# Filling the last stage's matrix products up to 128 rows and columns

## The chip, the cores and the metric

The kernel runs on one core of a Trainium2 chip. The metric is the device time of one execution in microseconds (us), as a median over runs. Beside it stands one profiled execution, from which every duration below comes. The engines are named as in the profile: PE is the matrix engine's multiplications, PEld its loads of the stationary operand, DVE the vector engine, ACT the scalar engine, POOL the GpSimd engine, SP the queue that issues the DMA transfers. In a matmul's shape, such as `64*128 64x96`, the first pair is the rows and columns of the array that the stationary operand fills, the second the moving operand.

## The reference

The input is `x` with 8 images of 64 by 64 pixels and 96 channels (C = 96), seen also as 8 sequences of 4096 tokens. Layer 0 is a state-space block with 192 inner channels (DI = 192); layer 1 is an attention without softmax and a small quantized network.

```
x = x + vss(group_norm(x))            # in_proj, 3x3 depthwise convolution, four selective scans,
                                      # y = layer_norm(y) * gamma + beta; y = y * silu(z)
                                      # out = y @ out_proj_w.T        (192 -> 96)
t = tokens(x)
t = t + attn(layer_norm(t))           # qkv = x @ Wqkv + bqkv; (q k^T) v for 6 heads; @ Wff + bff
t = t + ffn(layer_norm(t))            # q8(x) @ q8(W1) -> relu -> q8 -> @ q8(W2), 96 -> 384 -> 96
```

Without a softmax the attention is linear: q (k^T v) needs one product of the normalized tokens with themselves per sequence, the matrix `gram` of 97 by 97 with the constant 1 as a 97th channel, which carries the biases. It is multiplied with the weights into one matrix `weff` of 97 by 96, and each token's attention is one product with `weff`.

## The kernel before

Three stages follow each other: `pass1` (normalization, input projection, convolution), `pass2` (the scans, by far the longest) and `pass3`, which is what the change touches. `pass3` does everything from the layer norm after the scans to the output.

It works in units of 512 tokens (GRP), 8 units (UNITS) for each of 8 sequences, 64 in all. Inside a unit the tokens stand as 4 blocks (NU) of 128. A unit has a load and two parts:

- `load` (line 954) fetches the two scan directions `y` and `yo` with tokens on the partitions, the gate `zs` with channels on the partitions (128 channels in half 0, the remaining 64 in half 1), and the tokens `xr` for the residual.
- `first_part` (line 968) adds `y` and `yo` on POOL, standardizes on DVE, POOL and ACT (`standardize`, line 936), and transposes on PE: 4 transposes for channels 0 to 127 and 4 for channels 128 to 191 (64 columns of data). ACT copies each half out of PSUM with gamma and beta into `gt`, POOL multiplies it with `zs`. The product with `out_proj_w` runs, for each of the 4 blocks, over 128 rows with `w_out0` and then over 64 rows with `w_out1`, accumulating in the same PSUM tile. DVE adds the residual. The result is standardized into `ln` (96 channels, and POOL sets a 97th to 1), multiplied with itself into `pg`, and transposed into `lnT` (97 rows).
- `attention` (line 1021), once per sequence, makes `weff` from `pg`.
- `second_part` (line 1045), once the sequence's `weff` is there, multiplies `lnT` with `weff`, adds, standardizes into `lf`, transposes it into `xq` (96 rows, fp8), multiplies with `w1q` in three column blocks (`ph`), adds the bias and clips on DVE, quantizes on POOL (`hq`), multiplies with `w2q`, adds and stores.

A 32-bit product with `start`/`stop` as written appears in the trace as two matmul records with a stationary load each; a transpose is one record. So a unit has 16 records for `w_out`, 8 for `pg`, 8 for `weff`, 16 transposes (`tr`), 3 for `ph`, and 12 for `w2q`.

The order on each engine is fixed when the program is built. Each part is a generator that yields the engine and an assumed cost before each step; `weave` (line 142) plays all parts forward in assumed time and takes at each moment the step that could begin earliest. `InOrder` (line 83) chains the instructions of an engine in that order. At most five first and five second parts are open at a time (OPEN), and the second parts stand 12 units behind the first ones, so that the stage begins with first parts alone and ends with second parts alone. `Slots` and the tile pools count the buffers: 3 PSUM tiles for transposes, 2 for products, 2 for `ph`, 5 loads, 20 units held between the parts.

Of the kernel before, what the change touches and what calls it, by code (L numbers as in the profile page):

```python
# [33 lines left out]
F32 = mybir.dt.float32  # L34
F16 = mybir.dt.float16
BF16 = mybir.dt.bfloat16
F8 = mybir.dt.float8e5
AF = mybir.ActivationFunctionType
# [4 lines left out]
P = 128  # L43
NB, HH, WW, C = 8, 64, 64, 96
L = HH * WW
DI, N, R, K = 192, 16, 6, 4
# [12 lines left out]
GRP = 512  # L59
# [808 lines left out]
def pass3(ctx, tc, g, ident, mhalf, engines, y_d, z_d, out):  # L868
    nc = tc.nc
    pe, dve, act, pool = engines  # L870
    CA = C + 1
    sp = InOrder(tc, nc.sync)
    wp = ctx.enter_context(tc.tile_pool(name="p3w", bufs=1))
    one = ctx.enter_context(tc.tile_pool(name="p3one", bufs=1))
    two = ctx.enter_context(tc.tile_pool(name="p3two", bufs=2))

    OPEN = 5
    each = ctx.enter_context(tc.tile_pool(name="p3each", bufs=OPEN))

    LOADED, HELD = 5, 20  # L880
# [2 lines left out]
    held = ctx.enter_context(tc.tile_pool(name="p3held", bufs=HELD))  # L883
# [3 lines left out]
    ps_one = ctx.enter_context(tc.tile_pool(name="p3ps", bufs=1, space=PSUM))  # L887


    gb = wp.tile([P, 2, 2], F32, name="gb")  # L890
    for i, name in enumerate(("ln_gamma", "ln_beta")):
        nc.sync.dma_start(gb[:, 0, i : i + 1], g[name][0:P].unsqueeze(1))
        nc.sync.dma_start(gb[0 : DI - P, 1, i : i + 1], g[name][P:DI].unsqueeze(1))
    w_out0 = wp.tile([P, C], F32, name="w_out0")
    nc.sync.dma_start(w_out0, g["out_proj_wT"][0:P, :])
    w_out1 = wp.tile([DI - P, C], F32, name="w_out1")
    nc.sync.dma_start(w_out1, g["out_proj_wT"][P:DI, :])

    w_kv = wp.tile([CA, 2, C], F32, name="w_kv")
    nc.sync.dma_start(w_kv[0:C], g["Wqkv"][:, C:].rearrange("e (s c) -> e s c", s=2))  # L900
# [8 lines left out]
    nc.sync.dma_start(hmask, g["head_mask"])  # L909

    def load_quantized(shape, src, name):
        raw = one.tile(shape, F32, name=f"{name}_raw", tag="raw")
        nc.sync.dma_start(raw, src)
        q = wp.tile(shape, F8, name=name)
        nc.vector.tensor_copy(q, raw, saturate=False)
        return q

# [4 lines left out]
    nc.vector.tensor_copy(b1q, b1q8)  # L922
    b2q = load_quantized([P, C], g["b2"].unsqueeze(0).to_broadcast([P, C]), "b2q")

    NU = GRP // P
    UNITS = L // GRP
    done, counts = {}, {}
    loads, holds, grams, weffs = {}, {}, {}, {}

# [3 lines left out]
    def tokens(src, q):  # L933
        return src[q * GRP : (q + 1) * GRP].rearrange("(n p) c -> p n c", p=P)

    def standardize(src, dst, name, cost):

        yield "dve", 4 * cost
        st = each.tile([P, NU, 6], F32, name=f"st{name}")
        mv = each.tile([P, NU, 2], F32, name=f"mv{name}")  # L940
        for i in range(NU):
            dve.bn_stats(st[:, i, :], src[:, i, :])
        for i in range(NU):
            dve.bn_aggr(mv[:, i, :], st[:, i, :])
# [9 lines left out]
    def load(b, q):  # L954
        cols = slice(q * GRP, (q + 1) * GRP)
        end = yield "sp", 8.0, 5.0, slots["loaded"]
        y, yo = (loaded.tile([P, NU, DI], F32, name=name) for name in ("y", "yo"))
        for o, dst in enumerate((y, yo)):
            sp.dma_start(dst, tokens(y_d[b][o], q))
        zs = loaded.tile([P, 2, GRP], F32, name="zs")  # L960
        sp.dma_start(zs[:, 0, :], z_d[b][0:P, cols])
        sp.dma_start(zs[0 : DI - P, 1, :], z_d[b][P:DI, cols])
        xr = loaded.tile([P, NU, C], F32, name="xr")
        sp.dma_start(xr, tokens(g["x"][b], q))
        loads[b, q] = y, yo, zs, xr, slots["loaded"].taken
        done["load", b, q] = end

    def first_part(b, q):
        yield "load", b, q
        y, yo, zs, xr, of_loads = loads[b, q]  # L970
        yield "pool", 1.8, 0.3, slots["held"]
        t, lnT = held.tile([P, NU, C], F32, name="t"), held.tile([CA, GRP], F32, name="lnT")
        holds[b, q] = t, lnT, slots["held"].taken
        pool.tensor_add(y, y, yo)
        yield from standardize(y, y, "y", 0.45)
        for i, (ch, rows) in enumerate(((slice(0, P), P), (slice(P, DI), DI - P))):
            yield "pe", 0.6, 0.3, slots["tr"]
            pt, slot = take("tr", [P, GRP])
            for n in range(NU):
                pe.transpose(pt[0:rows, n * P : (n + 1) * P], y[:, n, ch], ident)  # L980
            end = yield ("act", 0.65) if i else ("act", 0.65, 0.3, slots["gates"])
            if i == 0:
                gt, of_gt = gates.tile([P, 2, GRP], F32, name="gt"), slots["gates"].taken
            act.activation(gt[0:rows, i, :], pt[0:rows, :], AF.Identity, bias=gb[0:rows, i, 1:2], scale=gb[0:rows, i, 0:1])
            slots["tr"].release(slot, end)
            yield "pool", 1.3
            pool.tensor_mul(gt[0:rows, i, :], gt[0:rows, i, :], zs[0:rows, i, :])
        end = yield "pe", 3.8, 0.3, slots["mm"]
        slots["gates"].release(of_gt, end)
        po, slot = take("mm", [P, NU, C])  # L990
        for i in range(NU):
            blk = slice(i * P, (i + 1) * P)
            pe.matmul(po[:, i, :], gt[:, 0, blk], w_out0, start=True, stop=False)
            pe.matmul(po[:, i, :], gt[0 : DI - P, 1, blk], w_out1, start=False, stop=True)
        end = yield "dve", 0.55, 0.0
        dve.tensor_add(t, po, xr)
        slots["mm"].release(slot, end)
        slots["loaded"].release(of_loads, end)
        ln = each.tile([P, NU, CA], F32, name="ln")
        yield from standardize(t, ln, "t", 0.35)  # L1000
        pool.memset(ln[:, :, C:CA], 1.0)
        if b > 0:
            yield "gram", b - 1
        end = yield "pe", 1.6
        if b not in grams:
            grams[b] = ps_one.tile([CA, CA], F32, name="pg")
        counts["gram", b] = counts.get(("gram", b), 0) + 1
        for i in range(NU):
            first, last = counts["gram", b] == 1 and i == 0, counts["gram", b] == UNITS and i == NU - 1
            pe.matmul(grams[b], ln[:, i, :], ln[:, i, :], start=first, stop=last)  # L1010
        if counts["gram", b] == UNITS:
            done["grams", b] = end
        yield "pe", 0.7, 0.3, slots["tr"]
        pl, slot = take("tr", [P, GRP])
        for i in range(NU):
            pe.transpose(pl[0:CA, i * P : (i + 1) * P], ln[:, i, :], ident)
        end = yield "act", 0.6
        act.copy(lnT, pl[0:CA, :])
        slots["tr"].release(slot, end)

    def attention(b):

        yield "grams", b
        end = yield "dve", 0.2
        gram = two.tile([CA, CA], F32, name="gram")
        dve.tensor_copy(gram, grams[b])
        done["gram", b] = end
        last = gram
        for rows, rhs, name in ((CA, w_kv[:, 1, :], "gv"), (C, w_kv[:, 0, :], "kvT"), (C, w_ff, "kvf"), (CA, None, "weff")):
            yield "pe", 0.7, 0.3, slots["mm"]  # L1030
            p, slot = take("mm", [P, NU, C])
            p = p[0:rows, 0, :]
            pe.matmul(p, last if rhs is not None else w_qT, rhs if rhs is not None else last, start=True, stop=True)
            end = yield "dve", 0.25
            last = two.tile([rows, C], F32, name=name)
            if name == "kvT":
                dve.tensor_mul(last, p, hmask)
            else:
                dve.tensor_copy(last, p)
            slots["mm"].release(slot, end)  # L1040
        dve.tensor_add(last[C:CA, :], last[C:CA, :], b_ff[C:CA, :])
        weffs[b] = last
        done["weff", b] = end

    def second_part(b, q):
        yield "weff", b
        t, lnT, of_hold = holds[b, q]
        end = yield "pe", 1.3, 0.3, slots["mm"]
        pa, slot = take("mm", [P, NU, C])
        for i in range(NU):  # L1050
            blk = slice(i * P, (i + 1) * P)
# [1 line left out]
        end = yield "dve", 0.55, 0.0  # L1053
        dve.tensor_add(t, t, pa)
        slots["mm"].release(slot, end)
        lf = each.tile([P, NU, C], F32, name="lf")
        yield from standardize(t, lf, "f", 0.35)

        yield "pe", 0.7, 0.3, slots["tr"]
        pf, slot = take("tr", [P, GRP])  # L1060
        for i in range(NU):
            pe.transpose(pf[0:C, i * P : (i + 1) * P], lf[:, i, :], ident)
        end = yield "dve", 0.7
        xq = each.tile([C, GRP], F8, name="xq")
        dve.tensor_copy(xq, pf[0:C, :], saturate=False)
        slots["tr"].release(slot, end)
        h1 = each.tile([P, NHC, GRP], F16, name="h1")
        for hc in range(NHC):
# [13 lines left out]
        po, slot = take("mm", [P, NU, C])  # L1082
# [17 lines left out]
    for b in range(NB):  # L1100
        units += [("first", b * UNITS + q - 12, first_part(b, q)) for q in range(UNITS)]
        units += [("load", b * UNITS + q, load(b, q)) for q in range(UNITS)]
        units.append(("attention", 0, attention(b)))
        units += [("second", b * UNITS + q, second_part(b, q)) for q in range(UNITS)]
    weave(units, {"load": 1, "first": OPEN, "attention": 1, "second": OPEN}, done)

# [44 lines left out]
```

## Time and profile before

| | |
|---|---|
| time, median of 3 runs | 10227.74 us (10223.3 to 10242.83) |
| time of the profiled execution | 10238.11 us |
| its span, first to last instruction | 10236.3 us |
| busy over the span: PE, PEld, DVE, ACT, POOL | 7669.6, 6320.8, 9578.9, 9152.3, 9194.7 us |
| mean clock granted to the matrix engine | 0.895 |
| last stage, from the last instruction of the scans | about 9331 to 10236 us of the span |

The page divides the span into 40 slices and gives for each the busy share of each engine in tenths and the clock that was granted to the matrix engine (1 is full). Times within the span are counted from the first instruction. All instructions that go through `InOrder` carry the line 91 of that helper, so groups are told apart by the names of their tiles: `mm<-w_out,gt` is the output projection, `tr<-ident,y` a transpose of `y`. Ends of matmuls are modelled; where the pace of a run of matmuls matters, it is read from the start of its first one to the start of the next group.

### The profile page before, as it was taken

How to read it: one execution, taken by the hardware profiler on the slowest of the kernel's cores; microseconds unless marked ns; L12 is line 12 of the kernel's file. 1: busy time of each engine (PE TensorE's matmuls, PEld its weight loads, DVE VectorE, ACT ScalarE, POOL GpSimd, SP SyncE). 2: the span in 40 equal slices, each digit the busy share in tenths (PEclk: the TensorE clock that was granted, in tenths of full speed). 3: DMA queues.
4: the chain of work that ended last, by engine and by line, in shares of the span. 5: the costliest groups of instructions: out<-in, count | busy, mean ns of one | idle time of the engine just before them, and what ended most of it. 6: DMA issues, size and time to landing. Idle time of an engine off the chain costs nothing.

```text
span 10236.3 us, 152471 instructions
## 1 busy us (share of the span) xinstructions
PE 7669.6 (75%) x52384; PEld 6320.8 (62%) x52384; DVE 9578.9 (94%) x6886; ACT 9152.3 (89%) x20499; POOL 9194.7 (90%) x3280
## 2 busy tenths in 40 slices
PE   7767777776777777777777777777777777776887
PEld 3336666665666666666666666666666666565775
DVE  7969999999999999999999999999999999996776
ACT  5669999999999999999999999999999999995665
POOL 1449999999999999999999999999999999997886
PEclk8889989989998989989989999999999899997776
DMA  5766776689976766799866666999667668996442
GB/s 165 236 209 217 229 228 221 228 209 206 211 221 212 224 218 216 223 205 205 221 210 223 219 214 225 209 204 213 216 213 230 210 226 210 206 208 169 125 126 60
DMA packets 928006, 2103.29 MB, mean 205 GB/s; under 512 B 274475, under 2 KB 422732, under 8 KB 925698
## 3 DMA queue, kind: packets, MB, share of 16 engines
q1 hardware_dynamic: 924426, 2092.18, 72.3%
q8 instruction: 420, 6.88, 0.3%
q14 instruction: 352, 2.88, 0.1%
q0 software_dynamic: 432, 0.94, 0.0%
q10 hardware_dynamic: 2376, 0.40, 0.0%
HBM read 1917.59 MB, written 175.66 MB: 204 GB/s over the span
## 4 chain that ended last, share of the span: by engine, by line
DVE 28%; ACT 26%; issue 15%; PE 15%; POOL 12%; DMA 3%; SPq 1%; DVEq 0%; ACTq 0%; POOLq 0%
DVE h L91 20%; ACT x L91 10%; ACT da L91 10%; POOL c L91 8%; PE acc L91 6%; DVE wide L91 5%; PE wide L91 3%; ACT L91 2%; PE mm L91 2%; PE px L91 1%; ACT y L91 1%; POOL xg L91 1%; PE pa L91 1%; DMA xd_d<-xd 1%; ACT delta L91 1%
## 5 line engine op out<-in xcount | busy, mean ns | idle before, releaser
L91 POOL TENSOR_TENSOR c<-c,h 128x2048 f32<-128x2048 f32 x1536 | 6958.0, 4555 | 299.2 <-issue 135.9
L91 DVE TENSOR_TENSOR_SCAN h<-da,carry,wide 128x1024 f32<-128x1024 f32 x2304 | 5268.2, 2332 | 137.6 <-PE wide L91 34.4
L91 ACT ACTIVATE x<-duT,bT 128x128 f32<-128x128 f32 (+1 forms) x13312 | 3970.3, 368 | 2.0
L91 PE MATMUL acc<-ident,c 128*128 128x128 f32 x24576 | 3438.8, 298 | 573.1 <-POOL c L91 566.2
L91 ACT ACTIVATE da<-delta,a_neg 128x1024 f32<-128x1024 f32 x3072 | 3513.1, 1144 | 315.2 <-DVE h L91 302.3
L91 PEld LDWEIGHTS acc<-ident,c 128*128 128x128 f32 x24576 | 3122.8, 155 | 1008.2 <-POOL c L91 893.7
L91 PE MATMUL wide<-ident,x 128*128 128x128 f32 x10752 | 1559.8, 291 | 646.4 <-DVE h L91 587.9
L91 PEld LDWEIGHTS wide<-ident,x 128*128 128x128 f32 x10752 | 1307.2, 150 | 841.5 <-ACT x L91 397.4
L91 DVE TENSOR_TENSOR_SCAN h<-da,wide 128x1024 f32<-128x1024 f32 x768 | 1712.8, 2271 | 45.1 <-PE wide L91 13.9
L91 DVE TENSOR_TENSOR wide<-du,wide 128x1024 f32<-128x1024 f32 x1280 | 1544.2, 1208 | 39.8 <-PE wide L91 29.4
L91 PE MATMUL wide<-xb,sel 96*128 96x512 bf16 x2560 | 820.6, 404 | 696.0 <-DVE h L91 689.1
L91 POOL TENSOR_TENSOR xg<-duT,bT 128x512 f32<-128x512 f32 (+1 forms) x640 | 893.8, 1412 | 28.4 <-PE wide L91 15.3
L91 PEld LDWEIGHTS <-sel 96*128 96x128 bf16 x2560 | 232.8, 102 | 876.4 <-DVE h L91 625.9
L91 PE MATMUL wide<-ident,xg 128*128 128x128 f32 x3584 | 482.6, 279 | 119.0 <-DVE h L91 117.4
L91 PEld LDWEIGHTS wide<-ident,xg 128*128 128x128 f32 x3584 | 411.7, 144 | 148.7 <-issue 110.0
L91 ACT ACT_TABLE_LOAD x385 | 494.0, 1283 | 6.9
L91 POOL TENSOR_TENSOR du<-delta,u 128x1024 f32<-128x1024 f32 x192 | 457.3, 2382 | 7.7 <-DMA u<-u_d 7.7
L91 DVE SCALAR_TENSOR_TENSOR u<-xpad,conv_w,u 128x4096 f32<-128x4096 f32 x96 | 452.7, 4716 | 1.9
L91 PE MATMUL px<-u,w_xp 128*128 128x512 f32 x512 | 253.6, 636 | 61.9 <-ACT u L91 43.0
L91 PE MATMUL mm<-w_out,gt 128*128 128x96 f32 (+1 forms) x1024 | 268.3, 383 | 32.7 <-POOL gt L91 16.1
L91 ACT COPY y<-acc 128x1024 f32<-128x1024 f32 x192 | 192.5, 1003 | 84.5 <-PE acc L91 84.1
L91 POOL TENSOR_TENSOR bq<-bq,bs 128x512 f32<-128x512 f32 (+1 forms) x48 | 121.7, 2536 | 161.4 <-ACT bs L91 140.3
(136 smaller groups left out, 6285.6 us busy)
## 6 DMA issues: line engine op xcount, KB each, us to landing
c<-xd_d SPq DMA_DIRECT2D x1024, 1024.0 KB
c<-xd_d SPq DMA_DIRECT2D x1024, 512.0 KB
u<-u_d SPq DMA_DIRECT2D x127, 512.0 KB
xdt<-dt_d SPq DMA_DIRECT2D x1146, 36.0 KB
xb<-b_d SPq DMA_DIRECT2D x382, 96.0 KB
u<-u_d SPq DMA_DIRECT2D x128, 256.0 KB
y_d<-y SPq DMA_DIRECT2D x24, 1024.0 KB
y<-y_d SPq DMA_DIRECT2D x64, 384.0 KB
```

The lines of the kernel that those rows point to most:

```text
L91: ins = getattr(self.engine, op)(*args, **kwargs).ins
```

## The change

Every product and transpose of the last stage is made to fill 128 rows of the array, and the transposes 128 columns. The 192 channels are cut into two overlapping halves, 0 to 127 and 64 to 191, and the first 64 rows of `w_out1` are zero, so that the channels that occur twice count once. `ln` and `lf`, which were taken from a pool for each unit, are five fixed buffers each, with 128 columns of which the ones behind the data are set once at the start of the stage: zeros, and the 97th of `ln` one. `weff` has its rows 97 to 127 set to zero, `w1q` its rows 96 to 127. The gate `zs` is loaded with 128 channels in both halves. The assumed costs and the steps of the parts are the same. In the built program the order on each engine is as before, but for memory sets: 15 more on POOL at the start of the stage and none (64 before) within the units, and 10 more on DVE.

```diff
-        nc.sync.dma_start(gb[0 : DI - P, 1, i : i + 1], g[name][P:DI].unsqueeze(1))
+        nc.sync.dma_start(gb[:, 1, i : i + 1], g[name][DI - P : DI].unsqueeze(1))
...
-    w_out1 = wp.tile([DI - P, C], F32, name="w_out1")
-    nc.sync.dma_start(w_out1, g["out_proj_wT"][P:DI, :])
+    w_out1 = wp.tile([P, C], F32, name="w_out1")
+    nc.vector.memset(w_out1[0:64], 0.0)
+    nc.sync.dma_start(w_out1[64:P], g["out_proj_wT"][P:DI, :])
+    lns = [wp.tile([P, NU, P], F32, name=f"ln{i}") for i in range(OPEN)]
+    lfs = [wp.tile([P, NU, P], F32, name=f"lf{i}") for i in range(OPEN)]
+    for i in range(OPEN):
+        nc.gpsimd.memset(lns[i][:, :, C:P], 0.0)
+        nc.gpsimd.memset(lns[i][:, :, C:CA], 1.0)
+        nc.gpsimd.memset(lfs[i][:, :, C:P], 0.0)
...
     def load_quantized(shape, src, name):
-        raw = one.tile(shape, F32, name=f"{name}_raw", tag="raw")
-        nc.sync.dma_start(raw, src)
-        q = wp.tile(shape, F8, name=name)
+        raw = one.tile([P, *shape[1:]], F32, name=f"{name}_raw", tag="raw")
+        if shape[0] < P:
+            nc.vector.memset(raw[shape[0] : P], 0.0)
+        nc.sync.dma_start(raw[0 : shape[0]], src)
+        q = wp.tile([P, *shape[1:]], F8, name=name)
...
-        sp.dma_start(zs[0 : DI - P, 1, :], z_d[b][P:DI, cols])
+        sp.dma_start(zs[:, 1, :], z_d[b][DI - P : DI, cols])
...
-        for i, (ch, rows) in enumerate(((slice(0, P), P), (slice(P, DI), DI - P))):
+        for i, ch in enumerate((slice(0, P), slice(DI - P, DI))):
...
-                pe.transpose(pt[0:rows, n * P : (n + 1) * P], y[:, n, ch], ident)
+                pe.transpose(pt[:, n * P : (n + 1) * P], y[:, n, ch], ident)
...
-            act.activation(gt[0:rows, i, :], pt[0:rows, :], AF.Identity, bias=gb[0:rows, i, 1:2], scale=gb[0:rows, i, 0:1])
+            act.activation(gt[:, i, :], pt, AF.Identity, bias=gb[:, i, 1:2], scale=gb[:, i, 0:1])
...
-            pool.tensor_mul(gt[0:rows, i, :], gt[0:rows, i, :], zs[0:rows, i, :])
+            pool.tensor_mul(gt[:, i, :], gt[:, i, :], zs[:, i, :])
...
-            pe.matmul(po[:, i, :], gt[0 : DI - P, 1, blk], w_out1, start=False, stop=True)
+            pe.matmul(po[:, i, :], gt[:, 1, blk], w_out1, start=False, stop=True)
...
-        ln = each.tile([P, NU, CA], F32, name="ln")
+        ln = lns[(b * UNITS + q) % OPEN]
         yield from standardize(t, ln, "t", 0.35)
-        pool.memset(ln[:, :, C:CA], 1.0)
...
-            pe.matmul(grams[b], ln[:, i, :], ln[:, i, :], start=first, stop=last)
+            pe.matmul(grams[b], ln[:, i, :], ln[:, i, 0:CA], start=first, stop=last)
...
-            pe.transpose(pl[0:CA, i * P : (i + 1) * P], ln[:, i, :], ident)
+            pe.transpose(pl[:, i * P : (i + 1) * P], ln[:, i, :], ident)
...
-        act.copy(lnT, pl[0:CA, :])
+        act.copy(lnT, pl)
...
-            last = two.tile([rows, C], F32, name=name)
+            full = two.tile([P if name == "weff" else rows, C], F32, name=name)
+            last = full[0:rows]
+            if name == "weff":
+                dve.memset(full[C:P], 0.0)
...
-        lf = each.tile([P, NU, C], F32, name="lf")
+        lf = lfs[(b * UNITS + q) % OPEN]
...
-            pe.transpose(pf[0:C, i * P : (i + 1) * P], lf[:, i, :], ident)
+            pe.transpose(pf[:, i * P : (i + 1) * P], lf[:, i, :], ident)
...
-        xq = each.tile([C, GRP], F8, name="xq")
-        dve.tensor_copy(xq, pf[0:C, :], saturate=False)
+        xq = each.tile([P, GRP], F8, name="xq")
+        dve.tensor_copy(xq, pf, saturate=False)
```

## The prediction

> **What bounds the kernel now.** The change touches the last stage only, about 905 us of the span. I read the table of busy time by stretch first, cutting the stage where the units change: first parts alone, both parts, second parts alone. Columns: stretch, its length, busy us (and instructions) of PE, PEld, DVE, ACT, POOL, granted clock, DMA share, GB/s.
>
> ```profile
> 9380.00:9510.00 130.00, 114.19 (x552) 92.90 (x552) 92.45 (x326) 78.91 (x168) 99.85 (x119) 0.68 0.50 149
> 9510.00:10080.00 570.00, 487.42 (x2873) 396.26 (x2872) 436.45 (x1582) 364.91 (x805) 470.12 (x534) 0.75 0.42 124
> 10080.00:10230.00 150.00, 114.08 (x619) 84.43 (x619) 94.42 (x337) 69.91 (x158) 85.01 (x97) 0.62 0.09 23
> ```
>
> PE is the busiest engine (88, 86, 76%), POOL next (77, 82, 57%), DMA far from full, and the clock is 0.62 to 0.75: PE runs at half speed for half of the time or more. The same view limited to `w_out` counts 210, 718 and 80 matmuls, at 16 a unit 13.1, 44.9 and 5 units: 9.9 us a first part in the first stretch, 12.7 us a unit in the second.
>
> Then the timeline of PE and PEld (start, length, engine, group, count, idle before). Two groups of `w_out`, at half and at full clock, with what follows them, and `weff` at half:
>
> ```profile
> 9724.43 5.33 PE L91 MATMUL mm<-w_out,gt 128*128 128x96 f32 x16
> 9729.69 1.17 PE L91 MATMUL tr<-ident,ln 128*97 128x128 f32 x4
> ```
> ```profile
> 9759.56 1.86 PE L91 MATMUL mm<-weff,lnT 97*128 97x96 f32 x8
> 9761.21 1.06 PE L91 MATMUL ph<-xq,w1q 96*128 96x512 fp8e5 x2
> ...
> 9764.01 3.09 PE L91 MATMUL mm<-w_out,gt 128*128 128x96 f32 x16
> 9767.03 0.93 PE L91 MATMUL pg<-ln 128*97 128x97 f32 x8
> ```
> ```profile
> 9756.77 0.50 PEld L91 LDWEIGHTS mm<-w_out,gt 64*128 64x128 f32 x2 [0.17 <-issue]
> ...
> 9759.34 1.83 PEld L91 LDWEIGHTS mm<-weff,lnT 97*128 97x128 f32 x8
> ```
>
> A record of `w_out` takes 5.26/16 = 0.329 us at half clock and 3.02/16 = 0.189 at full; one of `weff`, with equally large operands (128 columns loaded, 96 moving), 1.65/8 = 0.206. The loads of `weff` follow each other without a gap while those of `w_out` come in pairs with 0.17 us of idle between: where 128 and 64 rows alternate, loads aren't hidden behind matmuls.
>
> Last, PE and the clock in consecutive 3.41 us windows:
>
> ```profile
> 9725.83:9729.24 3.41, 3.41 (x11) 0.50 0.02 3
> 9732.66:9736.07 3.41, 3.41 (x12) 0.50 0.95 260
> 9736.07:9739.48 3.41, 3.41 (x16) 0.50 0.37 115
> 9739.48:9742.90 3.42, 3.42 (x27) 0.50 0.44 115
> 9742.90:9746.31 3.41, 2.88 (x29) 1.00 0.12 11
> ```
>
> PE is busy without a break, and the clock stays at half for three windows: busy time alone doesn't release it. I counted array cycles (moving columns, doubled for 32-bit; a `ph` of 512 columns takes 0.426 us at half, 1.2 cycles a ns). The third window has 1 `w_out` of 64 rows, 1 `ph`, 8 `weff`, 4 transposes: 192+512+1536+1024 = 3264 cycles, and the next stays at half. The fourth has 5 transposes, 8 `pg`, 12 `w2q`: 3984, and the next is full. Weighted by the rows filled, they have 2668 and 3984. Over the 252 windows of the stage, a threshold on plain cycles misjudges 20 next windows, one on row-weighted cycles 6, and it lies near 3,100 at either clock. So I take it that a window needs some 3,100 row-weighted cycles, 908 a us, to grant full clock next.
>
> [...]`weff` of 97 rows and 128 columns 0.206, `pg` of 97 columns 0.76/8 = 0.095 at full clock, so some 0.19 at half[...] here windows mostly of transposes do raise the clock.
>
> **The change part by part.**
>
> 1. `w_out` at one row count. [...]a record should run like `weff`: 0.206 at half, 0.103 at full. A unit saves 16·(0.329−0.206) = 1.97 us at half, 16·(0.189−0.103) = 1.38 at full. From below it is worth nothing, if the rows are not the cause; I take the full value.
> 2. `pg` loads 128 columns instead of 97: 8·(0.206−0.19) to 8·(0.206−0.165) dearer at half (cycles alone give 0.165), 8·0.01 at full: −0.3 and −0.1. The other products keep columns and pace; a transpose's 128 moving columns set its time already.
> 3. Sum on PE, with half clock for 64, 50 and 76% of the stretches (0.68, 0.75, 0.62): (13.1·1.52 + 44.9·1.48 + 5·1.58) = 94 us less work at today's clock.
> 4. The clock. Row-weighted cycles of a unit before: `w_out` 1536+768, transposes 4096, `pg` 1552, `weff` 1164, `ph` 1152, `w2q` 1152, together 11,420; after, 12,944. At half clock and without idling a unit takes PE 5.26+3.41+1.3+1.65+1.28+0.96 = 13.9 us, 823 cycles a us, under 908: half clock keeps itself. After, 12.2 us and 1,060: a saturated PE gets out of it. A first part alone (`w_out`, 12 transposes, `pg`) goes from 6,928 cycles in 5.26+2.56+1.3 us, 760 a us, to 7,696 in 3.3+2.56+1.65, 1,025. At full clock the second stretch's pace of 12.7 us gives 900 before and 1,020 after. Zeros count, I assume: identity matrices are nearly all zeros and transposes count in full. I expect 0.85 or more in the first two stretches.
> 5. POOL loses 64 sets of the one-column (112 ns, 7.2 us) in its queue; `pg` then waits for ACT alone (PE idled 5.3 us for them). It gains 15 sets at the start, 0.1 to 0.3 us each, in 20.08 us of idle before the first sum of `y`. They wait for buffers that the stored `y` of the scans held until about 9344, so 0 to 3 us of delay; I take 1. Without that cover they cost 1.5 to 4.5.
> 6. ACT and POOL on 128 rows instead of 64: free (770 against 775 ns; 1279 against 1291). Eight sets of `weff` rows on DVE stand before its copies, which wait for PE anyway: at most 2 us, were they not hidden. The fixed buffers add a wait of ACT for its own write of the same buffer five units earlier, long done; behind it would stand ACT's queue and `pg`. The order of every queue, SP's included, is else unchanged, so nothing is moved past a DMA issue.
> 7. `zs` brings 131 KB more for a unit, 8.4 MB: +9% on the 1.38 MB of a load. In the first stretch 149 GB/s becomes some 190 if that runs in 111 us; 245 was reached at 9360. Hidden behind five loads ahead; the first five would cost 3 us.
>
> PE then no longer bounds. POOL does: 98.7 us of work in the first stretch, 464.9 in the second. Now it is busy 77 and 82%, in the scans just before, as one of two bounds, 96%. I take 0.89, midway between the latter two, since its waits for DVE's `mvt` (29.8 us in the second stretch) and ACT's `gt` (14.4) shorten only as far as PE stood behind them: 98.7/0.89 = 111 (−19), 464.9/0.89 = 522 (−48). The tail is a chain of latencies at half clock, second parts giving 5,250 cycles in 8 to 11 us: −2. Start +1. Sum −68: the profiled 10238 becomes 10170, and the median, which stands 10 us lower, 10160.
>
> **Rivals.**
> - A[...] the clock doesn't rise, because rows of zeros don't count. Of the 94 us, PE's `mm` and `tr` hold about 30% of the chain in this stage: −28, about 10200. Against it: the identities.
> - B: the rows aren't why loads stay exposed (the halves also alternate two moving operands). `w_out` keeps its pace, `pg` is dearer by up to 0.33 a unit, off the path for the most part: +5 to +8, about 10235.
> - C, slower: the same, with PE on the path throughout at half clock: 64·0.33 = 21, with weights and start 26: about 10254. It decides from three quarters of that on the path. Against B and C: `weff` and `pg`, which also change operands each record, hide their loads.
> - POOL reaches 0.96: 103 and 484 us, −115 with the rest, about 10113: the lower end of the forecast.
>
> **How the numbers follow.** Forecast 0.65 (10110 to 10190, from a POOL share of 0.96 to 0.85), A 0.18, B 0.09, C 0.08. A difference of 0.2%, 20 us, is about what a measurement of this kernel can tell from no change. Faster 0.83 (forecast and A), same 0.09, slower 0.08. The range 10095 to 10220 takes in A and some better play than 0.96, and leaves B and C out.
>
> **What would show it.** Step 1: 16 `w_out` in 3.3 us at half clock and 1.7 at full, loads without gaps. Step 4: clock over 0.85 in the first two stretches, under 0.7 in the tail. Then POOL at 0.85 to 0.95, waits of DVE's `t` for PE's `mm` (87.1 us) at less than half. Wrong if `w_out` still takes 5 us, or the clock stays at 0.75 with PE under 70% busy.

## The result, and the profile after

| | before | after |
|---|---|---|
| time, median of 6 runs each | 10229.27 us | 10174.01 us (10170.3 to 10185.48) |
| time of the profiled execution | 10238.11 us | 10170.3 us |
| its span | 10236.3 us | 10168.5 us |
| mean clock granted to PE | 0.895 | 0.906 |
| last stage, from the last `y<-acc` copy to the end | 905.2 us | 849.9 us |

The ratio is 0.9945, with an interval of 0.9933 to 0.9958: the changed kernel is 55 us faster. Forecast were 10160 us and a range of 10095 to 10220. The two spans differ by 67.8 us, but 12.5 us of that arose in the scans, which the change does not touch; the last stage accounts for 55.3. That the profiled execution took 10170.3 us, as the prediction had it for this execution, is therefore luck: without the shorter scans it would have been some 12 us longer.

To compare stretch by stretch, both traces have to be cut at the same events, not at the same times. I cut at DVE's residual sums `t<-mm,xr`, one for each first part: from the first sum to the 13th (twelve first parts, almost alone), to the 58th (both parts), to the 64th, and to the end (second parts alone). The table of busy time by stretch of the kernel before, cut so (stretch, its length, busy us and instructions of PE, PEld, DVE, ACT, POOL, granted clock, DMA share, GB/s):

```profile
9371.07:9487.49 116.42, 99.41 (x470) 80.83 (x471) 78.41 (x272) 67.20 (x140) 88.69 (x105) 0.66 0.58 167
9487.49:10053.32 565.83, 484.27 (x2837) 393.02 (x2835) 434.76 (x1568) 361.99 (x799) 468.75 (x533) 0.75 0.43 125
10053.32:10133.01 79.69, 70.22 (x400) 56.25 (x399) 55.77 (x209) 48.46 (x109) 57.70 (x68) 0.74 0.15 40
10133.01:10236.33 103.32, 67.42 (x365) 47.53 (x363) 60.44 (x213) 41.28 (x93) 49.43 (x54) 0.55 0.10 27
```

The same table of the kernel after:

```profile
9359.05:9467.24 108.19, 79.08 (x471) 70.45 (x472) 76.39 (x273) 66.18 (x140) 88.11 (x93) 0.79 0.64 197
9467.24:9993.43 526.19, 400.00 (x2835) 343.71 (x2834) 435.26 (x1573) 361.03 (x799) 464.77 (x486) 0.86 0.49 146
9993.43:10066.06 72.63, 55.34 (x391) 46.84 (x389) 56.03 (x209) 48.56 (x109) 58.49 (x64) 0.87 0.16 46
10066.06:10168.50 102.44, 63.08 (x371) 44.69 (x371) 60.40 (x215) 41.32 (x93) 48.85 (x54) 0.64 0.10 27
```

The four differences are −8.2, −39.6, −7.1 and −0.9 us, and the piece before the first sum is 0.5 longer. PE has lost 124 of its 721 busy us, a part of that because the clock rose; DVE, ACT and POOL have the work they had. In the second stretch PE falls from 86 to 76% busy and POOL rises from 83 to 88%. In the first stretch POOL comes only from 76 to 81%: nothing is close to full there, so something other than an engine's work sets the pace.

The timeline of PE after shows the records themselves (start, length, group, count, idle before with its releaser): a group at full clock and the next one at half.

```profile
9401.16 1.80 PE L91 MATMUL mm<-w_out,gt 128*128 128x96 f32 x14 [1.54 <-POOL gt L91]
9402.80 1.06 PE L91 MATMUL pg<-ln 128*128 128x97 f32 x8
...
9409.70 3.30 PE L91 MATMUL mm<-w_out,gt 128*128 128x96 f32 x14 [1.70 <-POOL gt L91]
9412.79 1.92 PE L91 MATMUL pg<-ln 128*128 128x97 f32 x8
```

A group has 14 of a unit's 16 records, since two on half 0 run before the wait for `gt`. From the first record to the start of `pg` it is 1.64 us for 14 records at full clock and 3.09 at half, 0.117 and 0.221 us each; before, it was 0.189 and 0.329. Within a group the median distance of two starts is 112 and 213 ns, down from 187 to 205 and 319 to 351. The lists of waits (engine and tile, what it waited for: us in total, times, longest), first one line of before, then after:

```profile
DVE t L91 <- PE mm L91: 87.1, 60, 4.7
...
ACT y L91 <- DVE mvy L91: 95.9, 32, 20.4
PEld L91 <- POOL hq L91: 80.7, 46, 5.2
...
DVE t L91 <- PE mm L91: 31.0, 26, 2.3
```

DVE waits for the products 31.0 us in place of 87.1. What has grown is PE's own wait for POOL's quantized `hq` (52.5 before) and ACT's wait for DVE's `mvy` (84.1 before). PE now waits for POOL where DVE used to wait for PE.

### The profile page after: what moved, and what is told of

Its sections match the earlier page's. It is cut to its first block, busy times and chain, and to the rows that moved or that the text cites. A ratio compares the mean times of both kernels' runs of the same rounds, so it can differ in the third digit from the quotient of the medians.

```text
span 10168.5 us, 152388 instructions
## 1 busy us (share of the span) xinstructions
PE 7540.2 (74%) x52384; PEld 6239.7 (61%) x52384; DVE 9577.5 (94%) x6896; ACT 9175.2 (90%) x20499; POOL 9189.8 (90%) x3231
## 4 chain that ended last, share of the span: by engine, by line
ACT 29%; DVE 28%; issue 16%; POOL 12%; PE 11%; DMA 3%; SPq 1%; DVEq 0%; ACTq 0%; POOLq 0%
DVE h L91 20%; ACT x L91 11%; ACT da L91 11%; POOL c L91 7%; PE acc L91 6%; DVE wide L91 5%; ACT L91 2%; PE wide L91 2%; ACT y L91 1%; POOL xg L91 1%; PE px L91 1%; ACT delta L91 1%; PE pa L91 1%; DMA xd_d<-xd 1%; DVE u L91 1%
## 5 line engine op out<-in xcount | busy, mean ns | idle before, releaser
L91 PE MATMUL wide<-ident,du 128*128 128x128 f32 x1536 | 206.9, 278 | 67.6 <-DVE h L91 34.3
```

The lines of the kernel that those rows point to most:

```text
L91: ins = getattr(self.engine, op)(*args, **kwargs).ins
```

## The experiments

Of the kernels below, lengths of stages and stretches are from the profiled execution, cut at the same events; the ratios are of timed runs to the kernel before, with 95% intervals. There is one profile of each kernel, and in these eleven profiles the scans, the same in all, end between 9318.6 and 9336.8 us. So the length of the stage shows what a change does to it more clearly than the median does, but rests on one execution.

### The output projection alone

The part of the change that feeds and makes the output projection (transposes of `y`, `gt`, the gate `zs`, `w_out1`), with nothing else of it. In the expectations, D says that the time is lost at the change between 64 and 128 rows, K that the clock follows the rows filled. The main lines:

```diff
+    w_out1 = wp.tile([P, C], F32, name="w_out1")
+    nc.vector.memset(w_out1[0:64], 0.0)
+    nc.sync.dma_start(w_out1[64:P], g["out_proj_wT"][P:DI, :])
...
+        sp.dma_start(zs[:, 1, :], z_d[b][DI - P : DI, cols])
...
+        for i, ch in enumerate((slice(0, P), slice(DI - P, DI))):
...
+            pe.matmul(po[:, i, :], gt[:, 1, blk], w_out1, start=False, stop=True)
```

> The output projection alone filled to 128 rows (overlapping channel halves, zero rows in w_out1, zs with 128 channels in both halves); ln, lf, weff, xq, w1q and the set of the 97th column as before. Theory D+K ([...]the clock then rises): 16 w_out in 3.3 to 3.4 us at half clock, 1.8 at full; row-weighted cycles of a unit 12,188, at half clock in 11.9 us, 1,024 a us, over 908; clock about 0.83 in the stretch with both parts; 45 to 52 us less than before (10177 to 10184). Rival K (only the clock, by rows filled, matters): w_out still 5.2 us at half clock, about 15 us less. Rival M (the wait for the set in ln and the fixed buffers matter): no more than 10 us less.

Measured: 10183.04 us, ratio 0.9958 (0.9945 to 0.997), stage 852.2 us. Its first two stretches:

```profile
9369.46:9479.22 109.76, 79.87 (x469) 69.75 (x470) 75.30 (x273) 65.88 (x140) 88.64 (x105) 0.77 0.66 197
9479.22:10002.79 523.57, 396.99 (x2844) 341.62 (x2841) 438.13 (x1567) 359.90 (x799) 466.82 (x531) 0.83 0.50 147
```

Of the stage's 55.3 us, 53.0 are here; by the medians it is 44 of 55 us, and the two ratios' intervals overlap. The records follow each other at 213 and 112 ns, as in the full change.

### Everything but the output projection

The full change with the lines above put back, of which the diff shows one: fixed `ln` and `lf`, `pg` and `weff` on 128 rows and columns, `w1q` on 128 rows, POOL's sets at the start.

```diff
-            pe.matmul(po[:, i, :], gt[:, 1, blk], w_out1, start=False, stop=True)
+            pe.matmul(po[:, i, :], gt[0 : DI - P, 1, blk], w_out1, start=False, stop=True)
```

> The other half of the change: fixed ln and lf with zeros behind, weff, xq, w1q and transposes of 128, no set within the units; the output projection with 128 and 64 rows as before. Theory D+K: w_out stays at 5.2 us a group at half clock; row-weighted cycles 12,176 in some 14.2 us at half clock, 857 a us, under 908, so half clock still keeps itself; clock 0.76 to 0.79 with both parts; 3 to 12 us less than before (10217 to 10226). Rival K: most of the gain is here, 30 us or more less. Rival M: about 15 us less, from shorter waits of PE before pg.

Measured: 10235.54 us, ratio 1.0004 (0.9997 to 1.001), stage 908.9 us against 905.2.

```profile
9364.78:9486.22 121.44, 108.05 (x472) 89.30 (x471) 76.99 (x273) 67.85 (x141) 88.42 (x93) 0.63 0.57 162
9486.22:10051.20 564.98, 487.02 (x2835) 394.00 (x2834) 430.16 (x1574) 362.25 (x799) 466.73 (x488) 0.78 0.43 125
```

Without the output projection the rest brings nothing that can be measured, where 3 to 12 us had been expected. In the first stretch it even costs 5 us: PE is the busiest engine there, at 0.63 of the clock, and its `pg` now loads 128 columns (213 ns from record to record at half clock after, 165 before). The 49 sets fewer that POOL issues and the rows added to the other products do not show in the time. The output projection is the cause, and the next question is what about it.

### The two halves at 96 rows each

If what matters is that the two halves fill the same number of rows, two halves of 96 channels must do as well, without a zero row and without a byte more of `zs`. This is the kernel before with:

```diff
-    w_out0 = wp.tile([P, C], F32, name="w_out0")
-    w_out1 = wp.tile([DI - P, C], F32, name="w_out1")
+    w_out0 = wp.tile([C, C], F32, name="w_out0")
+    w_out1 = wp.tile([C, C], F32, name="w_out1")
...
-        for i, (ch, rows) in enumerate(((slice(0, P), P), (slice(P, DI), DI - P))):
+        for i, (ch, rows) in enumerate(((slice(0, C), C), (slice(C, DI), C))):
...
-            pe.matmul(po[:, i, :], gt[0 : DI - P, 1, blk], w_out1, start=False, stop=True)
+            pe.matmul(po[:, i, :], gt[0:C, 1, blk], w_out1, start=False, stop=True)
```

> The kernel before with its 192 channels cut into 96 and 96 instead of 128 and 64: no padding, nothing else. Row-weighted cycles of a unit stay at 11,420, as 96 and 96 rows have the mean of 128 and 64. Theory D[...]: 16 w_out in 3.3 to 3.4 us at half clock and 1.8 at full, loads without gaps; at half clock PE needs 11.9 us a unit, 960 cycles a us, a little over 908: clock about 0.80 with both parts; 35 to 45 us less than before (10184 to 10194). Rival K (rows filled alone): within 8 us of before, w_out still 5.2 us. Rival B of the prediction (alternating operands, not rows, expose the loads): w_out still 5.2 us, no change in time.

Measured: 10198.39 us, ratio 0.9973 (0.9962 to 0.9983), stage 864.5 us. The timeline of PE, a group at half clock and one near full:

```profile
9410.51 3.30 PE L91 MATMUL mm<-w_out,gt 96*128 96x96 f32 x14 [1.70 <-POOL ln L91]
...
9419.09 1.93 PE L91 MATMUL mm<-w_out,gt 96*128 96x96 f32 x14 [1.38 <-POOL ln L91]
```

The lengths are those of 128 rows (3.30 and, at full clock throughout, 1.80), so the lost time was not the empty part of the array. That it was the change between 128 and 64 rows, and not something in a record of 64 rows itself, the loads of the kernel before show, since each product makes two records of the same rows (PEld, at half clock):

```profile
9725.67 0.50 PEld L91 LDWEIGHTS mm<-w_out,gt 128*128 128x128 f32 x2 [0.17 <-issue]
9726.34 0.50 PEld L91 LDWEIGHTS mm<-w_out,gt 64*128 64x128 f32 x2 [0.17 <-issue]
```

and the same at 96 rows:

```profile
9410.51 3.06 PEld L91 LDWEIGHTS mm<-w_out,gt 96*128 96x128 f32 x14 [1.87 <-POOL ln L91]
```

Two loads of the same rows, 128 or 64, start 165 ns apart at half clock, and where the rows change it is 505 (108 and some 282 at full clock; all medians). A pair takes 670 ns, at equal rows 427: each change of rows costs some 240 ns at half clock and some 165 at full. What PE does in that time the trace does not show. The stretches:

```profile
9376.87:9485.43 108.56, 84.21 (x469) 74.58 (x470) 76.54 (x272) 65.89 (x140) 88.56 (x105) 0.72 0.65 181
9485.43:10023.22 537.79, 428.51 (x2837) 371.01 (x2835) 444.22 (x1568) 360.15 (x799) 468.02 (x531) 0.76 0.47 132
```

Equal row counts alone are worth 41 us of the stage; by the medians it is 29, where 35 to 45 had been expected. The clock, though, stays at 0.72 and 0.76, where the halves of 128 rows, half of one being zeros, had 0.77 and 0.83 with the same pace and the same moving columns. So in these runs rows counted for the clock, whatever stood in them.

A count over windows of 3.41 us, as in the prediction, says the same. (The clock in the trace is 0.5 or 1 and keeps its value for multiples of 3.413 us, in 797 stretches before and 769 after, all but the last one, which ends with the trace. A 32-bit column counts as two cycles: at half clock the 128 of a transpose take 213 ns, the 512 8-bit ones of `ph` 426.) Each window gets a number of array cycles, with one of several weights, and the best threshold is sought that tells from it whether the next window has full clock. The table gives the windows that this threshold misjudges, of 245 to 264 in each kernel (a record's cycles are spread from its start at the clock granted then, so that some counts differ a little from the prediction's):

| weight of a cycle | before | after | output projection alone | rest alone | 96 rows |
|---|---|---|---|---|---|
| rows filled, zeros counted | 5 | 6 | 7 | 5 | 5 |
| rows with data only | 5 | 13 | 25 | 15 | 5 |
| rows filled and columns loaded | 23 | 5 | 12 | 17 | 14 |
| none | 18 | 8 | 16 | 14 | 11 |
| rows filled, transposes left out | 65 | 53 | 57 | 70 | 76 |

With the first weight the thresholds of all five lie between 2,980 and 3,100 cycles; without a weight they run from 2,990 to 3,590. The last row shows that transposes count: without them 53 to 76 windows are misjudged.

The stage with 96 rows is 12 us longer than with the output projection filled up to 128. Every execution of the one was slower than every one of the other (15 us by the medians), though some of that lies in the scans. That these 12 us come from the clock is the likeliest reason but was not tested apart: the two kernels also differ in the transposes' columns, the size of `zs` and the rows that ACT and POOL work on.

### A clock raised without work

The full change, with `w_out` widened to 128 columns and `pg` moving all of `ln`: more moving columns, all zeros, so that more cycles are spent in the same records.

```diff
-    w_out1 = wp.tile([P, C], F32, name="w_out1")
+    w_out1 = wp.tile([P, P], F32, name="w_out1")
+    nc.vector.memset(w_out1[64:P, C:P], 0.0)
...
-            pe.matmul(grams[b], ln[:, i, :], ln[:, i, 0:CA], start=first, stop=last)
+            pe.matmul(grams[b], ln[:, i, :], ln[:, i, :], start=first, stop=last)
```

> The changed kernel with the moving side filled too: w_out0 and w_out1 widened from 96 to 128 columns with zeros, and ln whole as the moving operand of pg. Loads of 128 columns set these records' pace (0.213 and 0.110 us), so PE should take no longer, while a unit's row-weighted cycles go from 12,944 to 14,464. It asks what the clock is still worth. If the measure of activity is right, the clock rises from 0.79 to about 0.9 in the first stretch and from 0.86 to about 0.92 with both parts. If half clock still costs time now and then: 5 to 15 us less than the changed kernel. If PE is off the path at any clock: within 5 us of 10174.

Measured: 10177.98 us, ratio 0.9953 (0.9937 to 0.997), stage 847.1 us against 849.9 after.

```profile
9367.12:9475.27 108.15, 75.83 (x471) 64.47 (x472) 76.32 (x274) 65.80 (x140) 88.14 (x93) 0.87 0.65 199
9475.27:9996.45 521.18, 393.78 (x2840) 335.36 (x2839) 435.58 (x1573) 359.07 (x799) 464.21 (x486) 0.89 0.50 147
```

The clock goes from 0.79 to 0.87 and from 0.86 to 0.89, the pace of the records stays (PE is busy 394 us for 2840 records of the second stretch, 400 for 2835 after; already in the kernel after, the 128 moving columns of a transpose and the 96 of `w_out` both take 213 ns at half clock), and the time stays within the scatter (the second stretch is 5.0 us shorter, the third 2.5 longer). In the first stretch, 108.15 against 108.19 us: a faster PE is worth nothing there any more. Something else holds it.

### What holds the first stretch

The timeline of DVE and POOL after, in one first part of that stretch:

```profile
9403.62 1.81 POOL L91 TENSOR_TENSOR y<-y,yo 128x768 f32<-128x768 f32 x1
9403.69 1.76 DVE L91 SCALAR_TENSOR_TENSOR mvy<-mvy 128x4 f32<-128x4 f32 x1 [2.56 <-POOL mvy L91]
9405.37 0.55 DVE L91 TENSOR_TENSOR t<-mm,xr 128x384 f32<-128x384 f32 x1
...
9405.95 0.74 DVE L91 BATCH_NORM_STATS2 stt<-t 128x6 f32<-128x96 f32 x4
...
9407.06 0.23 POOL L91 TENSOR_SCALAR mvt<-mvt 128x4 f32<-128x4 f32 x1 [1.63 <-DVE mvt L91]
```

DVE's product for `mvy`, four elements a partition, takes 1.76 us and ends as POOL's sum of `y` ends. The same instruction when POOL stands still, from the timeline of the kernel before:

```profile
9414.44 0.16 DVE L91 SCALAR_TENSOR_TENSOR mvt<-mvt 128x4 f32<-128x4 f32 x1 [0.17 <-POOL mvt L91]
```

It needs 0.16 us. So POOL's own sum of `y` holds DVE, behind that queues the residual sum `t` (whose product was ready) with its statistics, and for these POOL then waits, 1.63 us in each unit of 8.53. It is so beside POOL's other large instructions. Of the 107 such products that begin in this stage beside a POOL instruction of 384 or more elements a partition, nearly all end some 20 ns after that one does (1.22 us is usual beside a product `gt`, 1.41 beside `hq`), while DVE's sum `t`, with one input from PSUM and one from SBUF, takes 0.54 us beside the sum of `y` and as much alone. Not every POOL instruction holds DVE: beside POOL's power of four elements a partition, 1.04 us long, the product keeps its 0.15. That the product is held because of its second SBUF input, and that one input and a scalar per partition would escape, was the author's estimate. The edit that tests it, in the helper that all three standardizations of a unit share, on the kernel after:

```diff
-        dve.scalar_tensor_tensor(mv[:, :, 0], mv[:, :, 0], -1.0, mv[:, :, 1], ALU.mult, ALU.mult)
+        for i in range(NU):
+            dve.tensor_scalar(mv[:, i, 0:1], mv[:, i, 0:1], mv[:, i, 1:2], -1.0, ALU.mult, ALU.mult)
```

> The changed kernel, with the one DVE operation in each standardization that multiplies two columns of mv from SBUF, 128x4, taken apart into four that multiply one column by a scalar operand. It asks what holds the first stretch at 8.5 us a unit where POOL has 6.8 us of work. Theory S: DVE's operation with two SBUF inputs waits for the POOL operation that runs beside it (1.2 to 1.8 us instead of 0.17), the sum and the statistics queued behind it come late, and POOL waits 1.6 us for them in each unit. Then the four take 0.3 to 0.5 us together, the first stretch runs at 7.0 to 7.6 us a unit, POOL is over 90% busy with both parts, and 20 to 35 us go beside the changed kernel (10139 to 10154). Rival: the operation only waits for its semaphore; then the four take 1.2 us or more and the time stays within 8 us of 10174.

Measured: 10157.16 us, ratio 0.9932 (0.9917 to 0.9947), stage 833.4 us, 16.5 less than after (20 to 35 us had been expected). The timeline of one first part:

```profile
9402.80 1.83 POOL L91 TENSOR_TENSOR y<-y,yo 128x768 f32<-128x768 f32 x1
9402.86 0.58 DVE L91 TENSOR_SCALAR mvy<-mvy 128x1 f32<-128x1 f32 x4 [3.21 <-POOL mvy L91]
...
9403.35 0.55 DVE L91 TENSOR_TENSOR t<-mm,xr 128x384 f32<-128x384 f32 x1
...
9405.04 0.23 POOL L91 TENSOR_SCALAR mvt<-mvt 128x4 f32<-128x4 f32 x1 [0.41 <-DVE mvt L91]
```

and its first two stretches:

```profile
9371.37:9466.64 95.27, 74.03 (x467) 66.77 (x468) 56.73 (x351) 65.51 (x140) 87.39 (x91) 0.83 0.74 226
9466.64:9984.99 518.35, 400.75 (x2849) 347.32 (x2848) 416.05 (x1972) 359.49 (x800) 468.54 (x488) 0.85 0.50 148
```

Four instructions finish in 0.58 us beside the same POOL sum, POOL's wait falls from 1.63 to 0.41, and the first stretch from 108.2 to 95.3 us, with POOL at 92%. What held the first stretch is shown, but not that a scalar in place of the second input is always enough: DVE's `h<-h,b1q`, 128x512 in f16 with a scalar per partition, takes 1.05 to 1.92 us beside a sum of `y` in the kernel after, and 0.34 alone.

### Was that wait there before?

The same edit on the kernel before tells whether the wait came with the change.

> The kernel before with the same DVE operation taken apart into four of one column. It asks whether that wait bounded the first stretch already, or took over when the output projection got faster. If PE at half clock bounds it (9.1 us of PE work in a first part against 8.5 us of the POOL and DVE chain), the first stretch stays within 5 us of its 116 us and the whole goes 0 to 15 us below the kernel before (10210 to 10227). If the wait bounded it too, the first stretch falls by 10 us or more and the whole by 15 to 30 us.

Measured: 10204.39 us, ratio 0.9974 (0.9964 to 0.9984), stage 876.4 us.

```profile
9366.50:9473.12 106.62, 94.91 (x463) 78.69 (x463) 57.09 (x351) 66.59 (x139) 88.23 (x103) 0.69 0.64 183
9473.12:10018.29 545.17, 467.64 (x2851) 380.92 (x2849) 420.30 (x1967) 362.06 (x800) 469.39 (x533) 0.78 0.44 130
```

Some 29 us of the stage, 9.8 in the first stretch and 21 with both parts. The case in which the wait bounded the kernel before too came true, the first stretch just under the 10 us asked of it. PE was the busiest engine, but not the only limit: shortening either its records (the output projection alone, −53 us) or this wait (−29 us) pays. The wait is not the change's doing; the change left it as what is next.

### The order of the work

The order of each queue is planned with assumed costs, and these still count PE's `w_out` at 3.8 us and `pg` at 1.6. On the kernel after:

```diff
-        end = yield "pe", 3.8, 0.3, slots["mm"]
+        end = yield "pe", 2.2, 0.3, slots["mm"]
...
-        end = yield "pe", 1.6
+        end = yield "pe", 1.1
```

> The changed kernel with the assumed costs that set the order brought to the measured pace: 2.2 for the output projection instead of 3.8, 1.1 for the product of ln with itself instead of 1.6. No instruction is added or taken away, only the order on the engines. If the order written for a slow PE holds POOL back, POOL goes from 88 to 91 or 92% busy with both parts and 10 to 20 us go beside the changed kernel (10154 to 10164). If POOL and DVE hold each other whatever the order, it stays within 8 us of 10174.

Measured: 10158.77 us, ratio 0.9932 (0.9917 to 0.9946), stage 827.4 us. The stretch of both parts is 22 us shorter, POOL 91% busy in it:

```profile
9479.07:9983.47 504.40, 395.38 (x2802) 337.78 (x2801) 417.92 (x1547) 355.17 (x789) 459.06 (x480) 0.86 0.51 152
```

An order made for a slow PE thus held POOL back, where the change left its order as it was. In the other direction, first parts standing nine units ahead of the second ones, in place of twelve (on the kernel after):

```diff
-        units += [("first", b * UNITS + q - 12, first_part(b, q)) for q in range(UNITS)]
+        units += [("first", b * UNITS + q - 9, first_part(b, q)) for q in range(UNITS)]
```

> The changed kernel with the second parts 9 units behind the first ones instead of 12. The stretches with one kind of part alone are the worst used (POOL 81% in the first, 48% in the tail of 102 us). Three units less in each: some 3 times 8.5 us less in the first and 3 times 8.5 in the tail, against 3 more units of 11.7 us with both parts: 15 us less than the changed kernel (about 10159). If the tail is one chain of a second part's latency, which it has whatever the number of units, within 6 us of 10174.

Measured: 10174.18 us, ratio 0.9949 (0.9934 to 0.9964), stage 849.7 us; 15 us less had been expected, and none came. The tail shrinks from 102.4 to 91.8 us, and the first two stretches give it back with 115.9 and 532.2 us in place of 108.2 and 526.2. The tail's latencies can be covered, but not for nothing.

Last, the two edits that helped together, the columns and the new costs:

> The changed kernel with both: the DVE operation in four of one column, and the order made with the measured pace of PE. One acts on the first stretch (13 us there alone), the other on the stretch with both parts (22 us alone). If they add: about 10140, 0.992 of the kernel before. If POOL is at its end anyway: 10150 to 10157, as each alone.

Measured: 10149.92 us, ratio 0.9921 (0.9908 to 0.9935), stage 812.6 us. In the first two stretches:

```profile
9371.97:9473.72 101.75, 80.31 (x509) 72.10 (x508) 65.24 (x390) 71.19 (x153) 92.81 (x99) 0.82 0.72 223
9473.72:9973.77 500.05, 387.20 (x2799) 335.58 (x2797) 401.41 (x1939) 355.02 (x787) 461.64 (x480) 0.86 0.51 153
```

It is the fastest of the kernels here by its median, 24 us below the changed one, though the two intervals overlap slightly. By the stage, the two edits on the kernel after give 16.5 and 22.5 us apart and 37.3 together: there they nearly add. The medians, 17 and 15 apart and 24 together, agree less well; they hold the scans too.

## Why the prediction was right, and where its sum was off

**Step 1, the pace of `w_out`: right.** A record was to go to 0.206 and 0.103 us, sixteen to 3.3 and 1.7; they follow each other at 213 and 112 ns, which gives 3.4 and 1.8. The kernel of 96 rows and the loads' spacing show the cause: it was the change to 64 rows and back, some 240 ns each time at half clock, not the unfilled array. Rival B, that the rows were not the cause, and with it rival C are refuted.

**Step 2, `pg` dearer: right.** From the start of one `pg` record to the next, 165 and 87 ns (medians) became 213 and 112, which is 0.4 and 0.2 us a unit for the 0.3 and 0.1 forecast. The transposes of `ln` kept their 213 and 109 ns when their columns went from 97 to 128. The kernel without the output projection shows where it costs: 5 us in the first stretch, with PE on the path at half clock.

**Step 4, the clock: the measure right, the sizes half so.** The clock was to be 0.85 or more in the first two stretches and under 0.7 in the tail. It is 0.86 with both parts and 0.64 in the tail, but 0.79 in the first stretch: the figure of 1,025 cycles a us was for a saturated PE, and there PE is 73% busy. Zero rows count in full, as was assumed (after, 6 windows are misjudged with them and 13 without); that excludes rival A, and it is probably the part of the gain, about 12 us, that two halves of 96 rows do not have.

**The share of POOL: right where both parts run, wrong where first parts run alone.** With both parts it is 464.77/526.19 = 0.883, forecast 0.89. Luck has a part in that: 0.89 was the middle of two shares seen elsewhere, not worked out from this stretch, and with another order of the same work the share is 0.91. The stretch's −48 came out as −39.6, and some of the rest stands in the next stretch (−7.1), since the prediction's cut at 10080 us reached into it. In the first stretch the forecast took the same 0.89, which by the cut used here gives 88.1/0.89 = 99 us; measured were 108.2 us at 0.814. This is the term that was mis-sized: some −17 us by this cut (−19 by the prediction's own) against −8.2, and it accounts for most of the difference between the forecast −68 and the measured −55. The sentence that failed is that POOL's waits for DVE's `mvt` shorten only as far as PE stood behind them: true, but in the first stretch most of that wait did not have PE behind it. POOL's waits in this stretch, before and after:

```profile
POOL mvt L91 <- DVE mvt L91: 22.0, 10, 4.6
...
POOL mvt L91 <- DVE mvt L91: 16.3, 10, 1.7
```

DVE was held by POOL's sum of `y`, and took 1.76 us for a product of 0.16. The row was in the profile before (count, busy us, mean ns, idle before):

```profile
L91 DVE SCALAR_TENSOR_TENSOR mvy<-mvy 128x4 f32<-128x4 f32 x64 | 50.2, 786 | 38.1 <-POOL mvy L91 38.0
```

786 ns on average for 512 elements; I read the wait and not the length of the instruction that it waited for.

**Step 3, the bound before: right as to PE's work, incomplete.** Taking these held products apart in the kernel before brings 0.26%, without any change to PE. So PE did not bound alone.

**Steps 5 to 7: right.** The list of POOL's instructions at the start of the stage, after:

```profile
9332.22 0.20 POOL L906 MEMSET ln<- 128x128 f32 x1 [18.40 <-DMA y_d<-y]
...
9334.01 1.80 POOL L91 TENSOR_TENSOR y<-y,yo 128x768 f32<-128x768 f32 x1
```

The 15 sets fill 1.7 us and the first sum of `y` follows at once; from the last copy of the scans to that sum it is 15.4 us, as before, so the delay was nearly nothing in place of 1 us. Copies and products on 128 rows cost what they cost on fewer: ACT's `gt<-tr,gb` takes 777 ns for both halves (775 and 770 before), POOL's `gt<-gt,zs` 1287 (1291 and 1279 before). The larger `zs` raises the first stretch to 197 GB/s at a DMA share of 0.64 (forecast 190) and stays hidden; with the columns edit the same stretch even draws 226.

**The tail: right.** −2 was forecast, −0.9 measured. It is a chain of latencies, which only another order shortened.

## What to carry to other kernels

Where matmuls alternate between row counts of 64 and 128, look at the gaps between the stationary loads: here equal row counts removed them (a pair of loads took 670 ns at half clock, then 427), and zero rows filled what was missing; they cost no time (3.30 us a group with 96 or 128 rows) and raised the clock (0.76 to 0.83 with both parts). Once PE was off the path, a still higher clock brought nothing (0.79 to 0.87, and 108.2 us either way). Before the gain of a faster engine is summed up, ask of the wait that is next why the instruction at its other end takes as long as it does; an instruction of 512 elements that takes 0.8 us on average here, and 0.16 when left alone, is being held by something. And where the order of the work was planned with costs, enter the new costs: that was worth as much here as the wait behind it.

## What the runs showed of the hardware that was not expected

- Whether the next window of 3.41 us has full clock follows the cycles weighted with the rows that an instruction occupies, zeros or not: the best threshold was 2,980 to 3,100 a window in five kernels, with 5 to 7 misjudged windows of some 250 each; taken apart in the kernel before, it is 3,040 for windows at half clock and 3,070 for those at full. Transposes count (53 to 76 misjudged without them).
- A change between records of 128 and 64 rows costs some 240 ns at half clock and some 165 at full; at half clock a `ph` of 96 rows is followed after 427 ns by another `ph` and after 426 by a transpose of 128 rows, so that change cost nothing.
- Between 96 and 128 moving columns a 32-bit record with 128 stationary columns keeps its pace (in the kernel after 213 and 112 ns for `w_out`, 213 and 109 for a transpose), so moving columns of zeros raised the clock of the first stretch from 0.79 to 0.87 at no cost, and there for no benefit.
- A DVE instruction of four elements a partition with two SBUF inputs takes 1.76 us beside a POOL sum of 1.81 us, and 0.16 without it; beside a POOL instruction of four elements, 1.04 us long, it keeps its length (0.15). Four instructions with a scalar in place of the second input take 0.58 in the same place.
